# Second attention of a four-layer kernel: maxima and scores on three shared pairs of PSUM banks, everything else in one bank

## Chip, cores and metric

The kernel runs on one core of a Trainium2 chip. The metric is the device time of one execution in microseconds (us), lower is better. The time before is 2225.94 us, the median of three runs (2224.97 to 2228.13).

## What is computed

Four layers in one launch, on x of 4 batches × 1024 tokens × 128 channels, all in fp32:

```python
x = x + L0_attn(layernorm(x))   # causal attention with a low-rank key, 16 heads
x = x + L0_ffn(layernorm(x))    # 8 experts, the best one of each token
x = x + L1_attn(layernorm(x))   # the second attention: the change lies here
x = x + L1_ffn(layernorm(x))    # 8 experts, two of each token, and a gate
```

The second attention has 16 heads of 8 channels. A query looks back over fixed offsets only (0 to 32, 48, 64, 96, 128 and 192), with a bias by offset and head:

```python
scores = einsum('bhnd,bhond->bhno', q, K_all) * scale + pos_bias.T[None, :, None, :]
scores = where(n_idx[:, None] < offs[None, :], -inf, scores)
out    = einsum('bhno,bhond->bhnd', softmax(scores), V_all)
return (out.flat * sigmoid(x @ Wgate.T + bgate)) @ Wout.T + bout
```

## The kernel before

The four layers follow one another as stages. The second attention takes from about 1358 to 1942 us of the profiled execution; its units run from 1402.9 us on.

**Units and blocks.** The work is cut into 16 units, each one batch and four heads. A unit has eight blocks of 128 tokens. Since no offset is above 192, the scores of a block of 128 queries need 320 keys, and a block of 128 keys serves 320 queries. The offsets that don't exist in that window are masked by a very negative bias (`by_query`, `by_key`). Softmax needs each query's maximum before the exponential, with queries on another axis than the one the values' matmul wants, so each unit goes through two passes:

- *maxima* (lines 1343 to 1364): for each block of queries and each of two "planes" `pl` (two heads each) two matmuls put 128 queries × 320 keys into PSUM (`sc`, line 1343), and VectorE adds the bias and takes the maximum in one instruction for each head (line 1350, `tensor_tensor_reduce`). It writes the sums back over `sc` and the maximum into `mxs`. When all eight blocks are done, `turn` transposes `mxs` (line 1359), ScalarE copies it negated into `mT` (line 1361), and four DMAs on SyncE's queue write it as extra rows into `qT` (line 1364), so that the second pass's matmul subtracts the maximum by itself.
- *attend* (lines 1426 to 1466): for each block of keys and each plane two matmuls put 128 keys × 320 queries into a pair of banks (`st`, line 1426); VectorE adds the bias (`sb`, line 1435), ScalarE takes the exponential (`pt`, line 1439), and one iteration later PE multiplies with the values into `av` (line 1451). ScalarE copies each finished block out (`avs`, line 1464), and VectorE clears it with a memset in half of the blocks (line 1466). Every four blocks, `normalized` transposes `avs` back (line 1381) and VectorE divides by the denominators (lines 1386 and 1387). After the fourth unit of a batch, `turned` (line 1400) and `projected` (line 1411) apply gate and output weights.

**Making a unit's operands.** `operands` computes `qT` and `kT` of the unit after next: four matmuls (line 1313), with a ScalarE copy for each `qT` half (line 1318) and two for each `kT` half (line 1324). Ahead of the first unit of a batch `shared` adds layer norm (line 1263 on GpSimd), its transposes (line 1267), the gate (lines 1279 and 1280) and `va` (lines 1284 and 1288). Units 2, 6 and 10 carry that work for units 4, 8 and 12.

**Order of the work.** PE's order is written out by hand (`manual_schedule`). One iteration of a unit (one block, both planes) puts on PE: one pair of maxima, the scores of plane 0 and plane 1, a second pair of maxima, one operand step, the values of the iteration before, a second operand step, and then whatever is due (transposes of `avs`, `turned`, `projected`, `turn`). The maxima run six steps ahead of the scores, so an iteration's two pairs belong to a later block or to the next unit. The other engines' orders come from a scheduler.

**PSUM.** It has eight banks of 512 fp32 a partition. `ps_s` holds two pairs of banks for `st` (line 1426); `ps_v` holds the one bank of `av`; `ps_1` holds three single banks that turn for everything else: each maxima matmul takes one of its own, and so do operands, transposes, gate, v, `turned`, `projected`, and the preparation of the last stage (`prepare_first`), whose helpers are handed `ps_1`. A pool gives the banks of a tag in turn, and the first instruction to write a bank waits until the readers of the tile before are done.

Of the kernel before, what the change touches and what calls it, by code (L numbers as in the profile page):

```python
# [10 lines left out]
F32 = mybir.dt.float32  # L11
# [5 lines left out]
PSUM = bass.MemoryType.PSUM  # L17

P = 128
# [30 lines left out]
HSLOT = 32  # L50
# [49 lines left out]
def fused_layers(ctx: ExitStack, tc: tile.TileContext, a: dict, out: bass.AP):  # L100
# [113 lines left out]
    class Room:  # L214


        def __init__(self, *rooms):
            self.rooms = [[r, 0] for r in rooms]

        def __call__(self, shape, dtype=F32):  # L220
            n = int(np.prod(shape[1:]))
            words = n if dtype != BF16 else (n + 1) // 2
            for room in self.rooms:
                r, at = room
                if at + words <= r.shape[1]:
                    room[1] += words
                    r = r[: shape[0], at : at + words]
                    r = r if dtype == F32 else r.bitcast(dtype)
                    axes = [f"a{k}" for k in range(len(shape) - 1)]
                    return r.rearrange(  # L230
                        f"p ({' '.join(axes)}) -> p {' '.join(axes)}",
                        **dict(zip(axes[1:], shape[2:])),
                    )
            raise ValueError(shape)

# [191 lines left out]
    with ExitStack() as ph:  # L429
# [3 lines left out]
        ps_s = ph.enter_context(tc.tile_pool(name="a_ps_s", bufs=2, space=PSUM))  # L433
        ps_v = ph.enter_context(tc.tile_pool(name="a_ps_v", bufs=1, space=PSUM))
        ps_1 = ph.enter_context(tc.tile_pool(name="a_ps_1", bufs=3, space=PSUM))
# [286 lines left out]
        def later(steps, do):  # L722
            due.append([steps, do])
# [80 lines left out]
        items = (4 * NPAIR, 8 * NPAIR)  # L804
        making = (None for b in range(B) for _ in operands(b))
        taking = (None for n in range(halves) for _ in maxima(*ready[n]))
        made = taken = 0

# [48 lines left out]
        for n in range(halves):  # L857
# [3 lines left out]
            def goals(p):  # L861

                if c == 0:
                    t1 = (n // 2 + 1) * sum(items)
                    return t0 + (t1 - t0) * min(1.0, p / 0.75), m0 + chunks * min(1.0, p / 0.95)
                now, ahead = min(1.0, p / 0.46), max(0.0, (p - 0.46) / 0.54)
                return (
                    t0 + items[0] * now + AHEAD * items[1] * ahead,
                    m0 + chunks * min(1.0, p / 0.38),
                )  # L870
# [5 lines left out]
            for k, w in enumerate(weights):  # L876
                done += w
                t, m = goals(done / span)
# [38 lines left out]
    with ph0 as ph:  # L917
        one = ph.enter_context(tc.tile_pool(name="f_1", bufs=1, reuse_waits="tile"))
# [3 lines left out]
        ps_1 = ph.enter_context(tc.tile_pool(name="f_ps_1", bufs=2, space=PSUM, reuse_waits="tile"))  # L922
# [303 lines left out]
    with ph1 as ph:  # L1226
        pk = ph.enter_context(tc.tile_pool(name="o_k", bufs=2, reuse_waits="tile"))
        pw = ph.enter_context(tc.tile_pool(name="o_p", bufs=2, reuse_waits="tile"))
        ps_s = ph.enter_context(tc.tile_pool(name="o_ps_s", bufs=2, space=PSUM, reuse_waits="tile"))
        ps_v = ph.enter_context(tc.tile_pool(name="o_ps_v", bufs=1, space=PSUM, reuse_waits="tile"))  # L1230
        ps_1 = ph.enter_context(tc.tile_pool(name="o_ps_1", bufs=3, space=PSUM, reuse_waits="tile"))


        av = ps_v.tile([P, 512], F32, tag="av")
# [95 lines left out]
        def maxima(n):  # L1330

            b, g = units[n]
            qT, kT = made[n]
            mxs = pw.tile([P, 4, NB], F32, tag="mxs")
            for i in range(NB):
                k0 = max(0, i * P - MAXO)
                w = (i + 1) * P - k0
                for pl in range(2):
                    scs = []
                    for hh in range(2):  # L1340
                        r0 = hh * 2 * HSLOT
                        sc = ps_1.tile([P, 512], F32, tag="ps1")
                        nc.tensor.matmul(  # L1343
                            sc[:, :w], qT[r0 : r0 + 2 * HSLOT, i * P : (i + 1) * P],
                            kT[r0 : r0 + 2 * HSLOT, pl, k0 : k0 + w], start=True, stop=True,
                        )
                        scs.append(sc)
                    for hh in range(2):
                        hl = 2 * hh + pl
                        nc.vector.tensor_tensor_reduce(  # L1350
                            scs[hh][:, :w], scs[hh][:, :w],
                            by_query[:, 4 * g + hl, :w][:, ::-1],
                            1.0, 2.0 * NEG, ALU.add, ALU.max, mxs[:, hl, i : i + 1],
                        )
                    yield

            def turn():
                ps = ps_1.tile([P, 512], F32, tag="ps1")
                nc.tensor.transpose(ps[: 4 * NB, :P], mxs.rearrange("p l i -> p (l i)"), ident)
                mT = pw.tile([4 * NB, P], F32, tag="mT")  # L1360
                nc.scalar.activation(mT, ps[: 4 * NB, :P], AF.Copy, scale=-1.0)
                for hl in range(4):
                    r = hl * HSLOT + HD
                    nc.sync.dma_start(
                        out=qT[r : r + 1, :].rearrange("o (i t) -> o i t", t=P),
                        in_=mT[hl * NB : (hl + 1) * NB, :],
                    )

            later(2, turn)

        def attend(n):

            b, g = units[n]
            qT, kT = made.pop(n)
# [44 lines left out]
            for kb in range(NB):  # L1419
                q0 = kb * P  # L1420
                w = min(WIN, T - q0)
                for pl in range(2):
                    st = ps_s.tile([P, 2, 512], F32, tag="st")
                    for hh in range(2):
                        r0 = hh * 2 * HSLOT
                        nc.tensor.matmul(  # L1426
                            st[:, hh, :w],
                            kT[r0 : r0 + 2 * HSLOT, pl, q0 : q0 + P],
                            qT[r0 : r0 + 2 * HSLOT, q0 : q0 + w],
                            start=True, stop=True,  # L1430
                        )

                    hs = slice(4 * g + pl, 4 * g + pl + 3, 2)
                    sb = pw.tile([P, 2, WIN], F32, tag="sb")
                    nc.vector.tensor_tensor(  # L1435
                        sb[:, :, :w], st[:, :, :w], by_key[:, hs, WIN - w :][:, :, ::-1], ALU.add
                    )
                    pt = pw.tile([P, 2, WIN], F32, tag="pt", bufs=4)
                    nc.scalar.activation(pt[:, :, :w], sb[:, :, :w], AF.Exp)  # L1439

                    def values(kb=kb, q0=q0, w=w, pl=pl, pt=pt):

                        cut = min(w, 512 - q0 % 512)
                        for lo, hi in ((0, cut), (cut, w)):
                            if lo == hi:
                                continue
                            for hh in range(2):
                                hl = 2 * hh + pl
                                hv = (4 * g + hl) * VW
                                c0 = (q0 + lo) % 512  # L1450
                                nc.tensor.matmul(  # L1451
                                    av[hl * VSLOT : (hl + 1) * VSLOT, c0 : c0 + hi - lo],
                                    va[:, kb, hv : hv + VSLOT],
                                    pt[:, hh, lo:hi],
                                    start=(kb == 0), stop=(kb == NB - 1),
                                    skip_group_check=True,
                                )
                        if pl == 1:

                            c, q = divmod(kb, 4)  # L1460
                            if q == 0:
                                avs[c] = pw.tile([P, 512], F32, tag="avs", name="avs")
                            cols = slice(q * P, (q + 1) * P)
                            nc.scalar.copy(avs[c][:, cols], av[:, cols])
                            if c == 0:
                                nc.vector.memset(av[:, cols], 0.0)
                            if q == 3:
                                later(2, lambda: normalized(c))

                    yield values  # L1470
# [44 lines left out]
        for n in range(len(units)):  # L1515
# [4 lines left out]
            for s in range(0, steps, 2):  # L1520
                next(maxs, None)
                two = [next(attending), next(attending)]
# [20 lines left out]
    with ExitStack() as ph:  # L1543
        one = ph.enter_context(tc.tile_pool(name="m_1", bufs=1, reuse_waits="tile"))
# [3 lines left out]
        ps_1 = ph.enter_context(tc.tile_pool(name="m_ps_1", bufs=2, space=PSUM, reuse_waits="tile"))  # L1548
# [185 lines left out]
```

## Time and profile before

The profile is one execution of 2226.58 us, with a span of 2224.8 us between its first and last instruction; the granted TensorE clock was 0.978 of full speed.

| | us |
|---|---|
| median of three runs | 2225.94 |
| profiled execution / its span | 2226.58 / 2224.8 |
| second attention, units only (1402.9 to 1940) | 537.1 |
| of that PE busy / weight loads | 514.2 / 300.4 |
| of that VectorE / ScalarE / GpSimd busy | 427.2 / 282.8 / 35.9 |
| line 1350, reduces of 320 elements: 384, mean | 0.506 |
| line 1350, accumulator reads: 512, mean | 0.141 |
| line 1435, additions of 640 elements: 192, mean | 0.817 |
| line 1439, exponentials of 640 elements: 192, mean | 0.736 |
| line 1313, operand matmuls: 128, mean | 0.641 |
| line 1324, copies into kT: 64, mean | 0.775 |

How to read it: PE is the matmul row, PEld its weight loads (they overlap the matmuls), DVE is VectorE, ACT ScalarE, POOL GpSimd, SP SyncE, whose queue (SPq) issues DMAs. A row of groups gives line, engine, operation, output <- input, partitions × elements, the count, then busy time and mean ns of one, then the engine's idle time just before these instructions and what ended most of it. A row of the timeline gives start, duration and the instruction, with the idle time before it in brackets. Matmuls are pipelined, so that a busy PE is not PE at its peak. The durations of one VectorE instruction and the next can overlap.

The units differ: from first score matmul to first score matmul of the next unit, most last 31.8 to 33.5 us, units 2, 6 and 10 last 39.8, 39.8 and 41.1, and unit 15, which has no maxima left to take, 18.1.

### The profile page before, as it was taken

What the parts mean: (1) busy time and instruction counts of PE and PEld (TensorE: products, weight loads), DVE (VectorE), ACT (ScalarE), POOL (GpSimd) and SP (SyncE); (2) the same over time, 40 slices, a digit from 0 to 9 for tenths busy, and PEclk for the clock granted to TensorE, in tenths of its full rate; (3) what the DMA queues carried; (4) which work ended last, traced back from release to release, by engine and by line L of the source; (5) the groups of instructions that cost most, each with busy time, mean ns of one, the idle gap of its engine ahead of it and who ended that gap; (6) DMA issues with size and microseconds to landing.
All of it is one profiled execution on the core that took longest, in us unless ns stands there. A gap on an engine that the chain in (4) does not pass through costs nothing. (4 is left out here: it accounts for less than half of the span.)

```text
span 2224.8 us, 31832 instructions
## 1 busy us (share of the span) xinstructions
PE 2048.0 (92%) x11540; PEld 1085.6 (49%) x11540; DVE 1345.9 (60%) x4098; ACT 923.8 (42%) x1491; POOL 443.8 (20%) x641
## 2 busy tenths in 40 slices
PE   5888999999999999999988887999999999989997
PEld 3654444444444444445335553555555555544453
DVE  5676746565555655555314343878778788674453
ACT  1112243344433444334543333454555545464553
POOL 3111122013210223013134543010000000151111
PEclk9999999999999999999999998999999999899998
DMA  3000000000000000020113220000000000031220
GB/s 68 1 1 1 1 2 1 2 1 1 1 1 1 1 1 1 6 79 28 36 37 109 77 56 18 2 1 2 2 1 2 1 2 2 13 97 55 86 82 15
DMA packets 52836, 49.84 MB, mean 22 GB/s; under 512 B 11555, under 2 KB 41480, under 8 KB 52680
## 3 DMA queue, kind: packets, MB, share of 16 engines
q1 hardware_dynamic: 48584, 40.90, 6.3%
q0 software_dynamic: 3216, 6.32, 1.1%
q8 instruction: 93, 1.52, 0.3%
q10 hardware_dynamic: 880, 0.57, 0.1%
q14 instruction: 63, 0.52, 0.1%
HBM read 39.85 MB, written 7.40 MB: 21 GB/s over the span
## 5 line engine op out<-in xcount | busy, mean ns | idle before, releaser
L707 ACT ACTIVATE pt<-st 128x1024 f32<-128x1024 f32 (+3 forms) x384 | 291.0, 808 | 381.9 <-PE st L700 376.3
L599 PE MATMUL sc<-kT,qT 64*128 64x512 f32 (+3 forms) x1536 | 412.5, 516 | 19.4 <-DVE mxs L615 9.6
L610 DVE CUSTOM_DVE_ANT_0 sc<-sc,cmask 128x512 f32<-128x512 f32 (+3 forms) x512 | 243.0, 512 | 142.0 <-PE sc L599 135.1
L700 PE MATMUL st<-qT,kT 64*128 64x512 f32 (+3 forms) x1536 | 309.9, 501 | 0.6 <-ACT pt L707 0.6
L599 PEld LDWEIGHTS sc<-kT,qT 64*128 64x128 f32 x1536 | 180.9, 189 | 199.6 <-DVE mxs L610 64.1
L1343 PE MATMUL sc<-kT,qT 64*128 64x320 f32 (+2 forms) x1024 | 261.3, 434 | 9.1 <-DVE mxs L1350 5.7
L1439 ACT ACTIVATE pt<-sb 128x640 f32<-128x640 f32 (+2 forms) x256 | 171.9, 683 | 217.2 <-DVE sb L1435 213.3
L1350 DVE CUSTOM_DVE_ANT_0 sc<-sc,by_query 128x320 f32<-128x320 f32 (+2 forms) x512 | 222.7, 473 | 53.4 <-PE sc L1343 50.8
L615 DVE TENSOR_REDUCE mxs<-sc 128x1 f32<-128x512 f32 x256 | 167.4, 687 | 116.6 <-PE sc L599 116.1
L711 POOL TENSOR_SCALAR_AFFINE_SELECT pt<-pt 128x256 f32<-128x256 f32 x256 | 102.9, 409 | 581.7 <-ACT pt L707 579.5
L700 PEld LDWEIGHTS st<-qT,kT 64*128 64x128 f32 x1536 | 151.6, 191 | 103.9 <-issue 68.8
L1426 PE MATMUL st<-qT,kT 64*128 64x320 f32 (+2 forms) x1024 | 191.0, 417 | 4.8 <-DMA qT<-mT 4.6
L1435 DVE TENSOR_TENSOR sb<-st,by_key 128x640 f32<-128x640 f32 (+2 forms) x256 | 182.3, 750 | 14.7 <-PE st L1426 12.0
L1343 PEld LDWEIGHTS sc<-kT,qT 64*128 64x128 f32 x1024 | 143.6, 186 | 82.9 <-DVE mxs L1350 31.6
L684 PE MATMUL av<-pt,va 128*32 128x512 f32 (+3 forms) x1536 | 168.5, 506 | 0.2 <-POOL pt L711 0.2
L1600 DVE TENSOR_TENSOR hd<-hd,wb 128x512 f32<-128x512 f32 x128 | 89.6, 710 | 101.8 <-ACT hd L1599 101.6
L1426 PEld LDWEIGHTS st<-qT,kT 64*128 64x128 f32 x1024 | 125.4, 189 | 31.5 <-DMA qT<-mT 9.9
L1699 PE MATMUL mT<-hd,ew 128*128 128x512 f32 x256 | 131.0, 595 | 2.7 <-DVE hd L1600 2.7
L1599 ACT ACTIVATE hd<-ps,eb 128x512 f32<-128x512 f32 x128 | 86.2, 686 | 103.6 <-PE ps L1594 91.7
L1594 PE MATMUL ps<-xnT,ew 128*128 128x512 f32 x192 | 98.0, 592 | 0.0
L1451 PE MATMUL av<-pt,va 128*32 128x320 f32 (+4 forms) x1280 | 90.9, 372 | 0.0
L954 DVE TENSOR_TENSOR hw<-sa,pg 128x512 f32<-128x512 f32 x46 | 31.6, 687 | 84.4 <-PE pg L949 75.8
(377 smaller groups left out, 2652.3 us busy)
## 6 DMA issues: line engine op xcount, KB each, us to landing
wb<-wt_d SPq DMA_DIRECT2D x64, 256.0 KB
w<-in_L_ffn_w SPq DMA_DIRECT2D x8, 512.0 KB
by_query<-bias_d SPq DMA_DIRECT2D x16, 160.0 KB
by_key<-bias_d SPq DMA_DIRECT2D x16, 160.0 KB
x<-in_L_attn_x SPq DMA_DIRECT2D x4, 512.0 KB
w<-in_L_ffn_w SPq DMA_DIRECT2D x8, 256.0 KB
ew<-in_L_ffn_ew SPq DMA_DIRECT2D x16, 128.0 KB
out<-mix SPq DMA_DIRECT2D x8, 256.0 KB
```

The costliest lines, as they stand in the source:

```text
L599: nc.tensor.matmul(sc[:, :n], qT[r0 : r0 + SLOT, pr, q * P : (q + 1) * P], kT[r0 : r0 + SLOT, pr, k0 : k0 + n], start=True, stop=True,)
L610: nc.vector.tensor_tensor_reduce(scs[hh][:, :n], scs[hh][:, :n], cmask[:, 512 - n :], 1.0, 2.0 * NEG, ALU.add, ALU.max, mx,)
L615: nc.vector.tensor_reduce(mx, scs[hh], AX.X, ALU.max)
L684: nc.tensor.matmul(av[hl * VSLOT : (hl + 1) * VSLOT, q0:], va[:, kb, h * VW : h * VW + VSLOT], pts[hl // 2][:, hl % 2, q0:], start=(kb == ...
L700: nc.tensor.matmul(st[:, hh, q0:], kT[r0 : r0 + SLOT, pr, kb * P : (kb + 1) * P], qT[r0 : r0 + SLOT, pr, q0:], start=True, stop=True,)
L707: nc.scalar.activation(pt[:, :, q0:], st[:, :, q0:], AF.Exp, scale=ATT_SCALE)
L1343: nc.tensor.matmul(sc[:, :w], qT[r0 : r0 + 2 * HSLOT, i * P : (i + 1) * P], kT[r0 : r0 + 2 * HSLOT, pl, k0 : k0 + w], start=True, stop=True,)
L1350: nc.vector.tensor_tensor_reduce(scs[hh][:, :w], scs[hh][:, :w], by_query[:, 4 * g + hl, :w][:, ::-1], 1.0, 2.0 * NEG, ALU.add, ALU.max, m ...
L1426: nc.tensor.matmul(st[:, hh, :w], kT[r0 : r0 + 2 * HSLOT, pl, q0 : q0 + P], qT[r0 : r0 + 2 * HSLOT, q0 : q0 + w], start=True, stop=True,)
L1435: nc.vector.tensor_tensor(sb[:, :, :w], st[:, :, :w], by_key[:, hs, WIN - w :][:, :, ::-1], ALU.add)
L1439: nc.scalar.activation(pt[:, :, :w], sb[:, :, :w], AF.Exp)
L1699: nc.tensor.matmul(mTs[k], ew2[:, e, f, :], hds.pop(n), start=False, stop=(s == steps - 1))
```

## The change

A small class takes the place of the pools `ps_s` and `ps_1`. It has seven banks: one single ("one") and three pairs (d0, d1, d2). `two()` gives the pair that was given least recently. `tile()`, which everything else calls, gives "one", unless "one" was the last that was given; then it takes a pair and uses its first bank.

```diff
+    class Banks:
+        def __init__(self, pool):
+            self.pool, self.given = pool, ["one", "d0", "d1", "d2"]
+
+        def give(self, tag):
+            self.given.remove(tag)
+            self.given.append(tag)
+            shape = [P, 512] if tag == "one" else [P, 2, 512]
+            return self.pool.tile(shape, F32, tag=tag, name=tag)
+
+        def two(self):
+            return self.give(next(t for t in self.given if t != "one"))
+
+        def tile(self, *_, **__):
+            return self.give("one") if self.given[-1] != "one" else self.two()[:, 0]
...
-        ps_s = ph.enter_context(tc.tile_pool(name="o_ps_s", bufs=2, space=PSUM, reuse_waits="tile"))
         ps_v = ph.enter_context(tc.tile_pool(name="o_ps_v", bufs=1, space=PSUM, reuse_waits="tile"))
-        ps_1 = ph.enter_context(tc.tile_pool(name="o_ps_1", bufs=3, space=PSUM, reuse_waits="tile"))
+        ps_1 = Banks(
+            ph.enter_context(tc.tile_pool(name="o_ps_1", bufs=1, space=PSUM, reuse_waits="tile"))
+        )
```

The maxima take one pair for the two heads of a plane, where they took two single banks; both matmuls and both reduces now work on the halves of one tile:

```diff
-                    scs = []
+                    sc = ps_1.two()
                     for hh in range(2):
                         r0 = hh * 2 * HSLOT
-                        sc = ps_1.tile([P, 512], F32, tag="ps1")
                         nc.tensor.matmul(
-                            sc[:, :w], qT[r0 : r0 + 2 * HSLOT, i * P : (i + 1) * P],
+                            sc[:, hh, :w], qT[r0 : r0 + 2 * HSLOT, i * P : (i + 1) * P],
                             kT[r0 : r0 + 2 * HSLOT, pl, k0 : k0 + w], start=True, stop=True,
                         )
-                        scs.append(sc)
                     for hh in range(2):
                         hl = 2 * hh + pl
                         nc.vector.tensor_tensor_reduce(
-                            scs[hh][:, :w], scs[hh][:, :w],
+                            sc[:, hh, :w], sc[:, hh, :w],
                             by_query[:, 4 * g + hl, :w][:, ::-1],
                             1.0, 2.0 * NEG, ALU.add, ALU.max, mxs[:, hl, i : i + 1],
                         )
```

And the scores:

```diff
-                    st = ps_s.tile([P, 2, 512], F32, tag="st")
+                    st = ps_1.two()
```

With it, the order of PE's instructions within the second attention stays as it was. On VectorE a few instructions change places (the memset of line 1466 against the maxima in one iteration of a unit, the second addition against two reduces in another, the layer norm's statistics in one unit). On ScalarE the head of the stage takes one more table load, and the second gate's sigmoid then comes after the next root. At the start of the last stage four hidden-layer matmuls come after the attention's last projections instead of between them.

## The prediction

> **What bounds the kernel now.** I read the shares first, then the groups of the second attention, its windows, and at last the timeline, iteration by iteration. The page says that PE works most and VectorE 60%; the groups that the change touches are lines 1343 and 1350 (maxima), 1426 and 1435 (scores).
>
> ```profile
> PE 2048.0 (92%) x11540; PEld 1085.6 (49%) x11540; DVE 1345.9 (60%) x4098; ACT 923.8 (42%) x1491; POOL 443.8 (20%) x641
> L1343 PE MATMUL sc<-kT,qT 64*128 64x320 f32 (+2 forms) x1024 | 261.3, 434 | 9.1 <-DVE mxs L1350 5.7
> L1350 DVE CUSTOM_DVE_ANT_0 sc<-sc,by_query 128x320 f32<-128x320 f32 (+2 forms) x512 | 222.7, 473 | 53.4 <-PE sc L1343 50.8
> L1426 PE MATMUL st<-qT,kT 64*128 64x320 f32 (+2 forms) x1024 | 191.0, 417 | 4.8 <-DMA qT<-mT 4.6
> L1435 DVE TENSOR_TENSOR sb<-st,by_key 128x640 f32<-128x640 f32 (+2 forms) x256 | 182.3, 750 | 14.7 <-PE st L1426 12.0
> ```
>
> That share is an average. The second attention runs from 1402.9 to 1940 us, and the windows show another limit there: in three plain iterations DVE is busy 9.26 of 10 us.
>
> ```profile
> 1656.00:1666.00 10.00, 9.96 (x87) 6.79 (x86) 9.26 (x29) 4.24 (x8) 0.00 (x0) 1.00 0.00 0
> ```
>
> (Columns: window, length, then busy time of PE, weight loads, DVE, ACT, POOL; clock; DMA share.) PE reads as busy too, but its matmuls overlap and wait inside the pipeline. The timeline of one iteration tells who leads:
>
> ```profile
> 1661.03 1.55 DVE L1435 TENSOR_TENSOR sb<-st,by_key 128x640 f32<-128x640 f32 x2
> 1662.49 0.49 DVE L1350 CUSTOM_DVE_ANT_0 sc<-sc,by_query 128x320 f32<-128x320 f32 x1
> 1662.90 0.14 DVE L1350 DVE_READ_ACCUMULATOR2_ANT mxs<- 128x1 f32 x1
> 1662.90 0.53 DVE L1350 CUSTOM_DVE_ANT_0 sc<-sc,by_query 128x320 f32<-128x320 f32 x1
> 1663.35 0.14 DVE L1350 DVE_READ_ACCUMULATOR2_ANT mxs<- 128x1 f32 x1
> ...
> 1663.66 0.17 DVE L1466 MEMSET av<- 128x128 f32 x1 [0.17 <-ACT avs L1464]
> ```
>
> DVE goes from the score additions (sb) to the two reduces with no gap; its one wait is 0.17 us ahead of the memset. The second reduce starts at 1662.90, together with the first one's accumulator read and before the first reduce ends (1662.49+0.49 = 1662.98). From first score matmul to first score matmul, the eight iterations of unit 9 last 6.00, 5.78, 3.63, 3.47, 3.34, 3.51, 3.31, 2.76 us, with DVE busy 3.49, 4.04, 3.38, 3.30, 3.17, 3.42, 2.95, 2.53. So the first two belong to PE (they hold the operand matmuls of a later unit), the next four to DVE. The unit's end belongs to a transfer: mT's four DMAs into qT, issued from 1738.74 on, release the next scores at 1742.70.
>
> **What the Trainium skill says.** "VectorE: DVE Perf Modes", section "Two Vector instructions with no wait between them": an operation that also writes out its accumulator is two instructions, the main one and a read. The trace agrees: 512 reduces and 512 reads (72.0 us, mean 141 ns). The same page, "The DRAIN you can't avoid": a semaphore between chained DVE operations costs nothing extra, 13.88 us for eight copies either way. The trace disagrees. Without a wait, a reduce's successor begins 0.08 us before the reduce ends; with a wait on DVE itself, as between line 1386 and line 1387, which reads its result, it begins some 0.035 us after the end (27 pairs of the trace read 0.034 or 0.035):
>
> ```profile
> 1703.32 0.26 DVE L1386 RECIPROCAL rden<-ps 128x16 f32<-128x16 f32 x1
> 1703.61 0.29 DVE L1387 TENSOR_TENSOR on<-ps,rden 128x128 f32<-128x128 f32 x1
> ```
>
> "PSUM — Partial Sum Buffer", "Engine vs sequencer instructions": updates attached to an engine's instruction fire when it completes, and VectorE's queue is strictly first in, first out. No row here contradicts that.
>
> **The change part by part.**
>
> *1. A pair for the maxima: DVE waits for itself.* Both reduces write their elementwise result over the tile that they read. With two tiles, each waited for its own matmul. With one tile for the pair, the program as built makes each second reduce wait for DVE's own count, which the first reduce's accumulator read advances. The second reduce therefore starts not with the read but after it: 0.141 + 0.035 = 0.176 us later. (Bounds: 0, if the wait hides; 0.083 + 0.035 = 0.118, if the reduce's own end counted; 0.176 is my value, since the read is what releases it.) Queued behind it on DVE are the second reduce, the next score addition, and so ACT's exponential and PE's values. 256 pairs make 45.1 us if none is covered. Which are? Of the 16 pairs of an ordinary unit, four lie in the two iterations of PE, and DVE has 2.5 and 1.7 us to spare there: hidden. Nine, from the third iteration to the first pair of the seventh, lie ahead of the addition that starts the unit's last chain (addition, exponential, values, copy, mT, DMA): 9 × 0.176 = 1.58 us. The last three lie beside the DMA: hidden. The waits for ACT ahead of the memset, about 0.17 us in three iterations, absorb 0.5; a memset that now comes ahead of the maxima in one iteration, and later starts of the first reduce (it now waits for both matmuls), give back 0.27. So 1.35 per ordinary unit, for the seven odd units 1 to 13: **+9.45**.
>
> *2. One bank for everything else.* Line 1313's operand goes into "one", the next into a pair, which stays taken until ACT's two copies of kT are done (0.775 us each). In ordinary units the next maxima already waited some 0.45 us for a bank (line 1343, from 1720.74 to 1721.58), so a later release there costs nothing new; without that cover it would be 0.44 us an iteration. In unit 0, +0.43 for this and 1.41 for its eight or so exposed pairs: **+1.8**. The head: the first operands need "one", which the second gate's sigmoid holds; ACT now does it after a table load, the root and another table load (1.28 us each), so the operands start some 3.6 us late (1372.95 before). PE then catches up on ACT, which had been the later one; 0.8 remains, and with the self-waits of the maxima's lead-in **+2.3**.
>
> *3. Units 2, 6, 10* carry the layer norm, gate and v of the next batch (39.8, 39.8, 41.1 us long against 31.8). There "one" goes round transposes, gate and v: the norm's transposes wait for a gate's sigmoid (+0.55), B's maxima wait until A's reduces are done, kT holds a pair. These holds make about 1.7, the self-waits of the iterations whose DVE is full 1.0: 3 × 2.7 = **+8.1**.
>
> *4. The rest.* Boundaries 3-4, 7-8 and 11-12 aren't set by the DMA (their last iterations last 3.84 us, not 2.76), so one pair's full wait counts: 3 × 0.5 = +1.5. Units 4 and 8 with the projections 2 × 1.2 = +2.4; unit 12, where DVE is busy 32.1 of 35.6 us, +1.9 (11 × 0.176); unit 14, 0.9 (5 × 0.176); transition to the last stage, whose first matmuls now follow the last projections, +0.5. Together **+7.2**.
>
> *5. What it gives.* Scores take turns on three pairs instead of two; the page shows only 4.8 us of waits of line 1426, nearly all for the DMA, so a third pair gains nothing while DVE leads. Unit 15 has no maxima and its iterations last 2 us for 1.36 to 2.3 of DVE: **−1.5** there. The transposes of mxs (line 1359) get a bank 0.5 us sooner, but mT must still follow the last exponential and avs copy: no gain.
>
> No DMA is added or moved past another. Sum: 9.45 + 1.8 + 2.3 + 8.1 + 7.2 − 1.5 = +27.4 us on the profiled execution's 2226.6, 2254; that lies 0.6 above the median of the runs, so **2253**.
>
> **Rivals.**
>
> *R1, faster.* DVE is busy for only 60%, line 1350's reduces waited 53.4 us for PE, and the self-wait vanishes in such gaps. Then the pairs help PE: unit 15 1.5, three mxs transposes 0.4 each, the split maxima 0.45 in 13 units, the lead-in 1.1: 9.7 gained, 2 to 5 lost to holds: 2220. The point that decides: a plain iteration must have 2 × 0.176 us of slack on DVE. The third to sixth have 0.09 to 0.25. That speaks against it.
>
> *R2, no difference.* The wait on DVE costs nothing, as the page on DVE says, and only the holds of "one" and the pairs count, 0.8 + 0.4 + 3 × 1.7 + 0.5, less 1.5 and small gains: +4, 2230. Against it stand the 27 pairs with 0.035 us after a wait; for it, that these aren't reduces.
>
> *R3, all exposed.* If PE's iterations lengthen too, since the late second reduce frees both banks of its pair late, 45 us and 8 of holds count, less 1.5: 2277. For it: lines 1343's loads wait for line 1350 in 31.6 us of the trace. Against it: three pairs give each reduce more than an iteration's half to finish.
>
> **How the numbers follow.** Forecast (2240 to 2266) 0.72; R3 0.12; R2 0.09; R1 0.05; 0.02 elsewhere. The range, 2232 to 2270, reaches part of the way to R2 and R3: it leaves out R1 and about half of either. A measurement can tell 0.2% (4.5 us: 2221.5 to 2230.4) from no change. Slower: the forecast, R3 and half of R2, 0.89; same: the other half of R2 and some of R1, 0.06; faster 0.05.
>
> **What would show it.** In the new trace the second reduce starts 0.17 us after its neighbour's accumulator read starts, not with it; the third to sixth iterations of ordinary units last about 3.7 to 3.9 us; the first two stay near 6.0 and 5.8. The norm's transposes wait for ACT's gate; score matmuls wait for ACT's kT. It is wrong if the second reduce still starts with the read (R2), if the iterations keep their length (R1), or if the first two grow by 0.35 each (R3).

## The result and the profile after

The changed kernel takes 2245.46 us, the median of five executions (2240.48 to 2250.86), against 2227.26 before in the same session. The ratio is 1.0085 with a 95% interval of 1.0065 to 1.0105, so slower by 19 us (14 to 23). The profiled execution took 2248.80 us (span 2247.1), 22.2 above the profiled one of before. The forecast was +27.4 us and 2253.

In the new page line numbers are 19 to 21 higher: 1343 became 1363 (maxima), 1350 is 1369 (reduces), 1426 is 1445 (scores), 1435 is 1454 (additions), 1313 is 1334 (operands), 1324 is 1345 (kT), 1464 is 1483 (avs), 1466 is 1485 (memset). The tiles are now called "one" and "d". The page's lines that answer to those shown of before:

```profile
PE 2036.5 (91%) x11540; PEld 1035.8 (46%) x11540; DVE 1362.8 (61%) x4098; ACT 928.1 (41%) x1492; POOL 440.8 (20%) x641
...
L1369 DVE CUSTOM_DVE_ANT_0 d<-d,by_query 128x320 f32<-128x320 f32 (+2 forms) x512 | 234.1, 461 | 66.8 <-PE d L1363 58.2
...
L1363 PE MATMUL d<-kT,qT 64*128 64x320 f32 (+2 forms) x1024 | 190.9, 450 | 36.8 <-DVE mxs L1369 34.7
...
L1454 DVE TENSOR_TENSOR sb<-d,by_key 128x640 f32<-128x640 f32 (+2 forms) x256 | 184.0, 750 | 8.5 <-PE d L1445 6.8
L1445 PE MATMUL d<-qT,kT 64*128 64x320 f32 (+2 forms) x1024 | 165.1, 422 | 8.5 <-ACT kT L1345 7.3
```

The work is the same; the waits aren't. PE now stands idle 36.8 us ahead of the maxima, nearly all for a reduce (9.1 before). The score matmuls' wait for the DMA has gone from the row, and one for ScalarE's kT stands there instead. The timeline of a plain iteration, VectorE alone, shows the wait that the sum rested on:

```profile
1741.05 0.49 DVE L1369 CUSTOM_DVE_ANT_0 d<-d,by_query 128x320 f32<-128x320 f32 x1
1741.45 0.14 DVE L1369 DVE_READ_ACCUMULATOR2_ANT mxs<- 128x1 f32 x1
1741.62 0.50 DVE L1369 CUSTOM_DVE_ANT_0 d<-d,by_query 128x320 f32<-128x320 f32 x1
1742.04 0.14 DVE L1369 DVE_READ_ACCUMULATOR2_ANT mxs<- 128x1 f32 x1
1742.21 0.17 DVE L1485 MEMSET av<- 128x128 f32 x1
1742.29 0.43 DVE L1369 CUSTOM_DVE_ANT_0 d<-d,by_query 128x320 f32<-128x320 f32 x1
```

The second reduce starts at 1741.62, 0.17 us after the read at 1741.45 and no longer with it. Over all 256 pairs the second reduce started with the read 210 times before, and 0.17 or 0.18 us after it 229 times now. This memset has no wait ahead of it any more; that will matter.

Stage by stage, from the two profiled executions (a unit is counted from its first score matmul to the next unit's, the last one to 2 us after the first score matmul of its last iteration):

| stretch | before, us | after, us | difference | forecast |
|---|---|---|---|---|
| start to the head | 1360.01 | 1358.47 | −1.5 | 0 |
| head, first layer-norm row (line 1263) to first scores | 42.92 | 46.56 | +3.6 | +2.3 |
| unit 0 | 29.82 | 32.22 | +2.4 | +1.8 |
| units 1 to 13, odd | 229.00 | 233.46 | +4.5 | +9.5, and 1.5 for boundaries |
| units 2, 6, 10 | 120.63 | 127.55 | +6.9 | +8.1 |
| units 4 and 8 | 66.52 | 70.86 | +4.3 | +2.4 |
| unit 12 | 35.64 | 37.56 | +1.9 | +1.9 |
| unit 14 | 37.80 | 37.10 | −0.7 | +0.9 |
| unit 15 | 18.13 | 18.22 | +0.1 | −1.5 |
| last stage | 284.35 | 285.09 | +0.7 | +0.5 |

Unit 14 can't be read to a microsecond: the granted clock fell to 0.83 and 0.84 in it. In either profile the first two iterations of one of units 2, 6 and 10 have such a stretch too (0.88 in unit 10 before, 0.89 in unit 6 after). Within an ordinary unit (9), the eight iterations:

| | 1 | 2 | 3 | 4 | 5 | 6 | 7 | 8 | sum |
|---|---|---|---|---|---|---|---|---|---|
| before | 6.00 | 5.78 | 3.63 | 3.47 | 3.34 | 3.51 | 3.31 | 2.76 | 31.78 |
| after | 5.27 | 6.11 | 3.48 | 3.67 | 3.33 | 3.72 | 3.45 | 3.52 | 32.54 |

### The profile page after: what moved, and what is told of

It is laid out like the page before. It is cut to its first block, busy times and chain, and to the rows that moved or that the text cites. A ratio compares the mean times of both kernels' runs of the same rounds, so it can differ in the third digit from the quotient of the medians.

```text
span 2247.1 us, 31923 instructions
## 1 busy us (share of the span) xinstructions
PE 2036.5 (91%) x11540; PEld 1035.8 (46%) x11540; DVE 1362.8 (61%) x4098; ACT 928.1 (41%) x1492; POOL 440.8 (20%) x641
## 5 line engine op out<-in xcount | busy, mean ns | idle before, releaser
L1369 DVE CUSTOM_DVE_ANT_0 d<-d,by_query 128x320 f32<-128x320 f32 (+2 forms) x512 | 234.1, 461 | 66.8 <-PE d L1363 58.2
L619 PEld LDWEIGHTS sc<-kT,qT 64*128 64x128 f32 x1536 | 181.0, 188 | 199.5 <-DVE mxs L630 64.1
L1363 PE MATMUL d<-kT,qT 64*128 64x320 f32 (+2 forms) x1024 | 190.9, 450 | 36.8 <-DVE mxs L1369 34.7
L720 PEld LDWEIGHTS st<-qT,kT 64*128 64x128 f32 x1536 | 151.7, 191 | 104.0 <-issue 68.6
L1454 DVE TENSOR_TENSOR sb<-d,by_key 128x640 f32<-128x640 f32 (+2 forms) x256 | 184.0, 750 | 8.5 <-PE d L1445 6.8
L1445 PE MATMUL d<-qT,kT 64*128 64x320 f32 (+2 forms) x1024 | 165.1, 422 | 8.5 <-ACT kT L1345 7.3
L1363 PEld LDWEIGHTS d<-kT,qT 64*128 64x128 f32 x1024 | 79.6, 185 | 125.6 <-DVE mxs L1369 96.1
L1445 PEld LDWEIGHTS d<-qT,kT 64*128 64x128 f32 x1024 | 95.8, 190 | 57.0 <-ACT kT L1345 19.8
```

The lines of the kernel that those rows point to most:

```text
L619: nc.tensor.matmul(sc[:, :n], qT[r0 : r0 + SLOT, pr, q * P : (q + 1) * P], kT[r0 : r0 + SLOT, pr, k0 : k0 + n], start=True, stop=True,)
L720: nc.tensor.matmul(st[:, hh, q0:], kT[r0 : r0 + SLOT, pr, kb * P : (kb + 1) * P], qT[r0 : r0 + SLOT, pr, q0:], start=True, stop=True,)
L1363: nc.tensor.matmul(sc[:, hh, :w], qT[r0 : r0 + 2 * HSLOT, i * P : (i + 1) * P], kT[r0 : r0 + 2 * HSLOT, pl, k0 : k0 + w], start=True, stop ...
L1369: nc.vector.tensor_tensor_reduce(sc[:, hh, :w], sc[:, hh, :w], by_query[:, 4 * g + hl, :w][:, ::-1], 1.0, 2.0 * NEG, ALU.add, ALU.max, mxs ...
L1445: nc.tensor.matmul(st[:, hh, :w], kT[r0 : r0 + 2 * HSLOT, pl, q0 : q0 + P], qT[r0 : r0 + 2 * HSLOT, q0 : q0 + w], start=True, stop=True,)
L1454: nc.vector.tensor_tensor(sb[:, :, :w], st[:, :, :w], by_key[:, hs, WIN - w :][:, :, ::-1], ALU.add)
```

## The experiments

A ratio is to the kernel before, run in the same session, with its 95% interval. Two causes had to be told apart: VectorE's wait for itself, and the banks (who holds "one" and the pairs).

### Wait and banks, one without the other

If the reduces write their elementwise sums, which nobody reads, into SBUF, then the tile they go to decides on the self-wait, whatever the banks are. This was done to both kernels. Four tiles in turn, so no wait:

```diff
                     for hh in range(2):
                         hl = 2 * hh + pl
+                        sums = pw.tile([P, WIN], F32, tag="sums", bufs=4)
                         nc.vector.tensor_tensor_reduce(
-                            scs[hh][:, :w], scs[hh][:, :w],
+                            sums[:, :w], scs[hh][:, :w],
```

For the version with the wait, the line with `pw.tile` stands ahead of `for hh`, so that both reduces of a pair write one tile. In the changed kernel `sc[:, hh, :w]` stands in place of `scs[hh][:, :w]`.

> The kernel before, but line 1350 writes its elementwise sums into SBUF scratch tiles (four in turn, nobody reads them) instead of back into PSUM; the maxima are the same. It is the base for its three companions: no wait between the two reduces of a pair. Both theories: near the kernel before, within 10 us either way; the reduce may take a little more or less with an SBUF output. Second reduces start with the accumulator read of the first.

> The kernel before, but the two reduces of a pair write their unread sums into one SBUF scratch tile, so that the second waits for VectorE's own first one, with the banks as before. Theory (the self-wait is the cause of most of the 19 us): 12 to 20 us slower than with the sums apart, second reduces 0.17 us behind the accumulator read. Rival (the banks are the cause: one bank for everything else, pairs held as a whole): 0 to 4 us slower.

> The changed kernel with its pairs of banks, but the sums of the reduces go into four SBUF scratch tiles in turn, so that no reduce waits for VectorE's own. Theory: the self-wait is gone, so 0 to 8 us slower than the kernel before with its sums apart (the holds of the single bank and of the pairs remain: I put them at 8, less 1.5 for the last unit). Rival: 15 to 20 us slower than that, about what the change costs.

> The changed kernel with the sums of a pair in one SBUF scratch tile: the self-wait is there again, without a write to PSUM. Theory: like the changed kernel, 12 to 20 us slower than with the sums apart. Rival: within 4 us of that with the sums apart. If the two causes need each other, both this and the one before with its sums shared differ from their sum.

| | no self-wait | self-wait |
|---|---|---|
| banks of before | 1.0004 (0.9992 to 1.0016) | 1.0051 (1.0033 to 1.0068) |
| banks of after | 1.0042 (1.0030 to 1.0053) | 1.0084 (1.0058 to 1.0109) |

Where the sums go costs nothing by itself (1.0004). The self-wait costs 0.0047 in the banks of before and 0.0042 in those of after, 10 and 9 us; the banks cost 0.0038 without it and 0.0033 with it, 8 and 7 us. So neither theory had it whole: wait and banks both count. Each of these differences is uncertain by 0.002 to 0.003, so the runs don't tell which is the larger. "Banks" here takes in the small changes of order on VectorE and ScalarE that came with them; no run separates these. For the banks I had 6.5 in my sum; for the wait, the other 21. The wait has not the same size in the four: the second reduce starts 0.23 us after the read's start in the second, 0.12 in the fourth, 0.17 in the changed kernel.

### Which holds

In the trace of the changed kernel, the waits of units 2, 6 and 10 name one: score matmuls, whose pair is still held by the two copies of kT. From the timeline of unit 2:

```profile
1500.62 1.45 ACT L1345 ACTIVATE kT<-d,b_qk,even 128x512 f32<-128x512 f32 x2 [0.74 <-PE d L1334]
...
1502.12 0.81 PE L1445 MATMUL d<-qT,kT 64*128 64x320 f32 x4 [0.58 <-ACT kT L1345]
...
1502.98 0.82 DVE L1454 TENSOR_TENSOR sb<-d,by_key 128x640 f32<-128x640 f32 x1 [0.50 <-PE d L1445]
```

The second scores start when the copies end (1502.07), and the addition stands idle for them, in an iteration that grew from 3.19 to 4.04 us. The other hold is in the head: the first operand matmul waits for the second gate's sigmoid, which stands behind two table loads of 1.28 us on ScalarE. It starts 16.48 us after the layer norm's first row instead of 12.94:

```profile
1374.21 0.69 ACT L1301 ACTIVATE gT<-one,b_gate 128x512 f32<-128x512 f32 x1
1374.95 1.53 PE L1334 MATMUL one<-xnT,w_qk 128*128 128x512 f32 x2 [3.58 <-ACT gT L1301]
```

Two edits to undo them, first one and then both:

```diff
-                    ps = ps_1.tile([P, 512], F32, tag="ps1")
+                    ps = ps_1.give("one") if j else ps_1.two()[:, 0]   # operands: kT in "one"
```
```diff
-                ps = ps_1.tile([P, 512], F32, tag="ps1")
+                ps = ps_1.two()[:, 0]   # gate
                 nc.tensor.matmul(ps, w_gate, xc, start=True, stop=True)
```

> The changed kernel with the two operand matmuls of line 1334 swapped over: the one for kT, which ScalarE holds with two copies, goes into the single bank, the one for qT into the first bank of a pair. Theory: the changed kernel's bank part, some 10 us without the self-wait, is in good part the hold of a pair by kT's copies, seen as score matmuls (line 1445) that wait for ScalarE's kT in the fourth and later iterations of units 2, 6 and 10, in 0, 4, 8 and 12 and in the second iteration of every other unit: 4 to 8 us faster than the changed kernel, that wait gone. Rival (three pairs in turn make the second maxima of an iteration wait for the first, and the head is late; the kT hold only fills idle time): within 2 us of the changed kernel.

> As the one before, and the two gate matmuls of line 1300 go into pairs too, so that the single bank isn't held by the gate's sigmoid behind two table loads. Theory: the operands of the first unit start some 3 us sooner, the head gives back 1 to 2.5 us, the units with shared work 0.5 each; 1 to 4 us faster than the one before. Rival: the held pair delays the first maxima as much: within 1 us.

> As the one before, and the sums of the reduces go apart into SBUF scratch, so that the self-wait is gone too. Theory (self-wait and holds are the whole cause): within 4 us of the kernel before with its sums apart (2222). Rival (the maxima's second pair waits for the first because both take the same pair of banks; that is left): 6 to 10 us slower than it, hardly better than the changed kernel with its sums apart (2232).

With the self-wait left in: 1.0072 (1.0051 to 1.0093) with kT's hold undone, 1.0067 (1.0050 to 1.0084) with both. That is within the intervals of the changed kernel, so these two alone decide nothing, although the waits for kT are gone from the trace (the fifth and sixth iterations of unit 2 last 5.29 and 3.24 us instead of 5.71 and 4.04).

With the self-wait gone as well: **0.9963 (0.9952 to 0.9974), 2215.23 us, faster than the kernel before.** Both sides of that expectation were off: this is 0.0041, or 9 us, below the kernel before with its sums apart (7 us by the medians of the two sessions). So the new banks gain something once nothing stands in their way. The windows show it in the head: the maxima ahead of the first unit take 19.97 us (25.62 before with sums apart). An ordinary unit takes 31.38 (31.71), but units 4, 8 and 12 together 105.0 (101.3), all at full clock, so that the units show no net gain. That the third pair is what helps the head is argued, not shown: no run took it away again.

The two holds by themselves, without the self-wait:

> The changed kernel with the sums apart (no self-wait) and kT's operand in the single bank; the gate stays there too. With both holds removed and no self-wait the kernel took 0.9963 of the time before, with neither removed 1.0042. Theory A (kT's hold is most of these 17 us): 0.997 to 0.999. Theory B (the gate's hold in the head is most of it): 1.002 to 1.004.

> The changed kernel with the sums apart and the gate in a pair; kT's operand stays in a pair. Theory A: 1.001 to 1.003, score matmuls still wait for kT's copies. Theory B: 0.997 to 0.999. If the two add up, this one and the one before lie together 0.0079 below twice 1.0042.

kT's hold undone: 0.9999 (0.9987 to 1.0011). The gate's undone: 0.9995 (0.9981 to 1.0009). From 1.0042, each gives about half of the 0.0079, and they add up (together 1.9994, expected 2.0005). By these ratios it is neither A nor B alone, but the granted clock differed: the executions with kT's edit ran at 0.972 to 0.979, those with the gate's at 0.980 to 0.982. In the 35 executions of the kernel before in that session, 0.001 of clock went with about 1.9 us (2216.98 us at 0.984, 2234.39 at 0.975). Brought to one clock with that, an estimate, kT's edit gives some 12 us and the gate's 5, which is near Theory A. The traces point the same way:

| time saved against the changed kernel with its sums apart, us | kT's edit | the gate's edit |
|---|---|---|
| head, first layer-norm row to first scores | 3.7 | 6.0 |
| unit 0 | 1.4 | 0.0 |
| the ten units at full clock in all three (1, 3 to 5, 7 to 9, 11 to 13) | 3.6 | 0.6 |
| fifth and sixth iterations of units 2, 6 and 10, at full clock | 4.7 | 0.0 |

The gate's edit lets the first maxima start 17.6 us after the layer norm's first row instead of 22.5; kT's takes 0.32 us off the second iteration of an ordinary unit (6.11 to 5.79). Why the clocks differ, no run shows.

### How much of the self-wait counts

> Both holds removed, and the sums of a pair in one SBUF scratch tile: a self-wait of 0.12 us a pair (with the read's 0.083 us instead of 0.141), nothing else changed from the version at 0.9963. Theory (once the holds are gone, the self-wait is half exposed, 0.174 us a pair having cost 21 us): 12 to 17 us slower than that version, 2227 to 2232. Rival (the 21 us came from the write to PSUM, not from the wait): within 4 us of 2215.

Measured: 2222.61 us, 1.0005 (0.9994 to 1.0017), so 0.0042 or 9 us for 256 waits of 0.12 us, 30 us in all. The forecast (12 to 17) was too high, the rival too low. A bit under a third counts. The iterations say how: each from the second to the seventh is longer by 0.12 us, the price of *one* wait, and not of two. So which?

> Both holds removed, sums in SBUF; only the first pair of maxima of an iteration (plane 0) shares its scratch tile and so has the self-wait of 0.12 us, the second has none. Theory: the loop of an iteration runs from the first pair's reduces over the second pair's matmuls (same pair of banks), values, the copy to avs and the memset back to the first pair's reduces, so only the first pair's wait counts; the second one's falls into the gap ahead of the memset. Then this takes nearly all of what both waits take (0.0042 of the time): 1.002 to 1.004 of the version without waits, 2220 to 2224 us, and each of the second to seventh iterations of an ordinary unit is 0.12 us longer. Rival (both count half, because VectorE is the bound): half of it, 0.06 us an iteration.

> The counterpart: only the second pair (plane 1) has the self-wait. Theory: within 0.001 of the version without waits (2213 to 2218 us), iterations unchanged, and the idle time of VectorE ahead of the memset shorter by about 0.12 us; only the maxima ahead of the first unit, which have nothing between them, may lose about 1 us. Rival: half of what both take, 0.002 (about 2220), 0.06 us an iteration.

```diff
-                        sums = pw.tile([P, WIN], F32, tag="sums", bufs=4)
+                        if hh == 0 or pl == 1:   # e12: pl == 0
+                            sums = pw.tile([P, WIN], F32, tag="sums", bufs=4)
```

| self-wait | ratio (interval) | iterations 1 to 8 of an ordinary unit | sum |
|---|---|---|---|
| none | 0.9963 (0.9952 to 0.9974) | 5.70 5.79 3.24 3.53 3.20 3.58 3.21 3.13 | 31.38 |
| both pairs | 1.0005 (0.9994 to 1.0017) | 5.37 5.91 3.36 3.65 3.32 3.71 3.34 3.46 | 32.12 |
| first pair | 1.0001 (0.9991 to 1.0011) | 5.37 5.91 3.36 3.66 3.32 3.70 3.34 3.46 | 32.12 |
| second pair | 0.9972 (0.9962 to 0.9982) | 5.70 5.79 3.24 3.54 3.20 3.58 3.21 3.13 | 31.38 |

The rows are those of unit 9, that of both pairs of unit 1; in unit 9 of that kernel the eighth iteration lasts 3.69 and the sum is 32.34. In the second to seventh iterations the first pair's wait counts in full, the second's not at all. Two timelines from the exponentials to the memset, first without a wait:

```profile
1721.59 1.47 ACT L1459 ACTIVATE pt<-sb 128x640 f32<-128x640 f32 x2 [1.90 <-DVE sb L1455]
1722.14 0.48 DVE L1370 CUSTOM_DVE_ANT_0 sums<-d,by_query 128x320 f32<-128x320 f32 x1
...
1722.55 0.48 DVE L1370 CUSTOM_DVE_ANT_0 sums<-d,by_query 128x320 f32<-128x320 f32 x1
...
1722.96 0.25 ACT L1484 COPY avs<-av 128x128 f32<-128x128 f32 x1
1723.31 0.17 DVE L1486 MEMSET av<- 128x128 f32 x1 [0.27 <-ACT avs L1484]
```

and with the wait in the second pair alone:

```profile
1723.98 1.47 ACT L1460 ACTIVATE pt<-sb 128x640 f32<-128x640 f32 x2 [1.90 <-DVE sb L1456]
1724.53 0.48 DVE L1371 CUSTOM_DVE_ANT_0 sums<-d,by_query 128x320 f32<-128x320 f32 x1
...
1725.06 0.49 DVE L1371 CUSTOM_DVE_ANT_0 sums<-d,by_query 128x320 f32<-128x320 f32 x1
...
1725.35 0.25 ACT L1485 COPY avs<-av 128x128 f32<-128x128 f32 x1
...
1725.70 0.17 DVE L1487 MEMSET av<- 128x128 f32 x1
```

From the first exponential to the memset it is 1.72 us in both. The second pair's reduces run beside the exponentials and the copy to avs, which stands in ScalarE's queue right behind them; the memset waits for that copy. In the first, VectorE was idle for 0.27 us there, and the wait of 0.12 falls into it. The loop that sets the length is: first pair's reduces, two additions, second exponential, copy, memset, first pair's reduces. My expectation had the loop go through the second pair's matmuls and the values instead; they end earlier (1722.31 for the values), so that part of it was wrong. All waits of the memset for the copy in the second attention, one line of the waits of each kernel, without a wait, with the first pair's, with the second pair's:

```profile
DVE av L1486 <- ACT avs L1484: 29.7, 57, 2.0
```
```profile
DVE av L1487 <- ACT avs L1485: 29.7, 57, 2.0
```
```profile
DVE av L1487 <- ACT avs L1485: 18.8, 24, 1.9
```

(us in total, times, the longest.) The first pair's wait leaves that idle time as it was; the second's takes 33 of the 57 gaps away, 10.9 us. In the changed kernel it is 17.1 us in 21 gaps. The one place where the second pair's wait was expected to count, the maxima ahead of the first unit, lasts 20.78 us with it and 19.97 without.

## Why the prediction was right, and where it was not

**Direction and range held**, at +19 us for +27, and so did the mechanism and its price: 0.174 us a pair for 0.176, from the accumulator read and the 0.035 us behind it. (The trace of before has 28 pairs with that 0.035, not 27.) The closeness of the sum is in part luck: the odd units with their boundaries, units 2, 6 and 10 and unit 14 came out 9.3 us below their forecasts, the head and units 0, 4, 8 and 15 5.4 above.

**The exposure of the self-wait was too high.** The prediction said: "Nine, from the third iteration to the first pair of the seventh, lie ahead of the addition that starts the unit's last chain", 1.35 us for each odd unit after corrections. Measured: 0.76 in unit 9, 0.64 on average. I took a VectorE with a busy share of 0.93 and a gap of 0.17 us as one queue that any delay lengthens. It has two halves: ahead of the additions a wait counts, behind them it runs beside ScalarE's exponentials. Five of the nine pairs lie in the first half (the first pairs of the third to seventh iterations): 5 × 0.174 = 0.87 us. Unit 9 of the changed kernel is 0.84 longer than with its sums apart (31.70). The trace of before already had the sign of it: the memset's wait for avs, which I had entered as 0.5 us to be absorbed in three iterations and not as the mark of another queue on the path.

**The sign in the iterations came only by half.** The third to sixth were to last 3.7 to 3.9 us. The fourth and sixth do (3.67 and 3.72); the third and fifth are no longer than before (3.48 and 3.33). With the sums apart in both, the new banks shorten these two from 3.63 and 3.36 to 3.24 and 3.20, and the changed kernel's are then 0.24 and 0.13 longer. That the banks would do this the prediction did not have.

**The extra waits at the boundaries 3-4, 7-8 and 11-12 didn't come.** Units 3, 7 and 11 grew by 0.59, 0.76 and 0.60, no more than the others.

**The holds were right in kind, but for one.** The prediction named the late operands of the head (3.6 us; measured 3.54; it had grown to 5.3 at the first maxima, and the stretch from there to the first scores then ran 1.7 faster), the copies of kT and the gate. The transposes of the layer norm were to wait for a gate's sigmoid; this did not come. Every wait ahead of them (line 1288) that names another engine is for GpSimd, 37.9 us in 40 (37.7 in 40 before). It said that kT's hold costs nothing new in ordinary units. With the self-wait there, that is so to 0.1 us (second iteration 6.11, and 6.02 without the hold); without it the hold costs 0.32. Hold and self-wait cover one another in part, which fits that removing the holds alone gave 0.0018 (not told from nothing), and removing them after the self-wait 0.0079.

**The third pair's gain was put in the wrong place.** Unit 15 was to gain 1.5 and gained nothing: its shorter iterations, of about 2 us, hold 1.24 us of scores and 0.75 of values, so PE fills them. The gain lies in the maxima ahead of the first unit, where R1 had 1.1 us: 5.6 without wait and holds, 1.7 in the changed kernel.

**The rivals.** R1 (the change is faster) is false for the change as it is, and true for it with three short edits more: 0.9963. R2 took VectorE's wait on itself for free, as the Trainium skill, "VectorE: DVE Perf Modes", section "The DRAIN you can't avoid", has it for copies; 229 pairs with 0.17 us say otherwise here, and the first pair's wait alone moved the time by 0.0038. R3 (all exposed) is refuted by the second pair's run.

**Open.** With the sums in PSUM and both holds undone, the self-wait costs 0.0104, or 23 us, of 256 × 0.174 = 45; with the sums in SBUF 0.0042 of 256 × 0.12 = 30. The longer wait of the first pair explains part, and the granted clock, lower by 0.002 in the former, perhaps 3 us more by the estimate above. Whether writing the sums to PSUM costs something of its own in the new banks is open: that it costs nothing (1.0004) was measured in the old ones only. Also not traced is what covers the second pair's wait in iterations without a memset, though the last table shows that it is covered there too.

## What to carry to other kernels

Putting two tiles that one engine works on in turn into one tile can make the engine wait for itself; look at what the built program waits for, and give the unread output a place of its own. Before pricing a wait by a busy share, split the engine's iteration at its waits for other engines: here only the half that no other engine ran beside counted. And a bank is held until its slowest reader is done (here two copies of 0.77 us, and a sigmoid behind two table loads), so choose who takes which bank: two such choices were worth 0.0079 of the time here once the self-wait was gone. Where effects are this small, compare the granted clocks of the runs before dividing the gain among causes.

## What was not expected of the hardware

- The accumulator read of line 1350 takes 0.141 us when the instruction's other output goes to PSUM, and 0.083 when it goes to SBUF (512 each). Where a wait hangs on the read, that is a third of its price.
- A second reduce that waits for PE and for VectorE itself starts 0.144 us after the read's end (banks of before with the sums shared), one that waits for VectorE alone 0.035.
